# One maximum over two heads, scatters in twos, and norms recorded later, in a six-layer decoder kernel

## The chip, the cores and the metric

The kernel runs on one core of one Trainium2 chip. The metric is the device time of one execution in microseconds (us): the median of three runs. A separate execution was profiled; durations, waits and stretches of time come from that one. The core's engines run their own queues in order: TensorE (PE) for matmuls, VectorE (DVE), ScalarE (ACT), GpSimd (POOL), and SyncE (SP), which only issues transfers.

## The reference

Sixteen batches of 128 tokens with 512 features pass through six sublayers, each followed by a residual add and a layer norm: a state-space scan, a cross attention with heads of 128, a ternary feed-forward, and then the three that matter here.

```
# 4: causal self-attention, 16 query heads of 32 on 4 key heads, 8-bit activations, ternary weights
p = softmax(where(causal, -inf, q k^T / sqrt(32)));  x = norm(x + bitlinear(p v, Wo))
# 5: gated cross attention, 16 heads of 32, masked keys
p = softmax(where(mask, q k^T / sqrt(32), -inf));    x = norm(x + sigmoid(n wg) * ((p v) wo))
# 6: experts: 8 of 64 masks per token by softmax and top-k, grouped into 8 weight sets
w = top8(softmax(x gate));  per set g: xg = x + softmax(w_g) mask_up[g]
x = norm(x + sum_g sum(w_g) * (silu(xg G_g) * (xg U_g)) D_g)
```

## The kernel before, in words

The six sublayers are written as stages. The two small-head attentions share one stage, `stage_attention`. It makes eight `SelfAttention` objects and then eight `GatedAttention` objects, one for each pair of batches, and cuts each into eight units of four heads: unit `n` is batch `n // 4`, key head (or row group of 32 partitions) `n % 4`. A loop over a step number `t` records, for the units at several distances ("lags") from `t`, the pieces of a small pipeline:

- `scores(n)`, two steps ahead and for even `n` only: PE adds the mask by a matmul and multiplies queries and keys of two units, row groups side by side, into two PSUM tiles of one bank each, tagged `sc0` to `sc3`. `Side` keeps these matmuls in the written order, the second unit first.
- `top(n)`, one step ahead: DVE takes the maximum over keys of the four heads of one unit (L1001, L1170) and multiplies it by a negative scale (L1002, L1171).
- `exps(n)`: ACT makes four exponentials (L1010, L1178). In the self-attention POOL then adds up parts of the rows (L1013, L1014), which the values' step sums (L1043). In the gated one `norm(n)` follows: two small DVE steps (L1184, L1185), and POOL multiplies the whole unit (L1186).
- `turn(n)`: four transposes on PE into the only bank of the pool `ppt`, and a copy to SBUF, for odd `n` on ACT (L1025), for even `n` on DVE (L1027).
- `values(i)` after four units: PE multiplies by the values. In the self-attention ACT copies the result (L1041), DVE sums and inverts the row parts (L1043, L1044), PE turns it back and DVE scales it (L1050). In the gated one the output matmul follows, DVE multiplies by the gate (L1211), POOL adds it to the residual `x` (L1212), and after the second batch of a pair DVE makes the layer norm (`layernorm`, L61 to L72, whose first instruction is L68).

Python generators, advanced once per step (`yield`), hold the projections, values and outputs; so a `yield` sets at which step an instruction is recorded. That recording is not the final order: a scheduling layer below it places the instructions on each engine's queue, and only `Side` pins some of them.

From the middle of the gated attention on, `Moe` runs beside it. `route(p)` decides for one pair of batches of the first half which experts each token goes to; ACT copies the tokens into a row buffer `r_row` (L1453, four buffers, so two pairs), DVE fills in the weights (L1475 to L1477), and `scatter` (L1481) sends each of the two rows to eight expert buckets in DRAM by indirect transfers from POOL's queue (L1486), one per step. The second half of the batches is routed during the expert stage, `stage_moe`.

The expert stage loops over 98 tiles of 128 tokens, each a unit with fetch, masks, gate and up products, and the product with `dn` into `y`, which DVE copies to `yo` (L1549) and ACT's queue stores to DRAM. `combine` later gathers the results back (L1558, POOL's queue), and after three steps POOL adds them to `x` (L1565). After two steps more, for the last expert of the first half, `finish` makes a pair's final layer norm on DVE and sends the result out.

Of the kernel before, what the change touches and what calls it, by code (L numbers as in the profile page):

```python
# [10 lines left out]
F32 = mybir.dt.float32  # L11
# [5 lines left out]
ALU = mybir.AluOpType  # L17
AX = mybir.AxisListType
PSUM = bass.MemoryType.PSUM

P = 128
NB = 16
D = 512
KC = D // P
# [836 lines left out]
class SelfAttention:  # L861
# [4 lines left out]
    HD = 32  # L866
    SCALE = 1.0 / math.sqrt(HD)
    LAG = 1

    def __init__(self, k, p, pools):  # L870
        self.k, self.nc, self.xs = k, k.nc, k.x[2 * p : 2 * p + 2]
        self.wk, self.wr, self.pp, self.psc, self.ppt, self.pao = pools
        self.o, self.part, self.sT, self.s, self.sc, self.mx = [], [None, None], {}, {}, {}, {}

    def rope(self, ps, n, tag):
        nc, HD, tabs = self.nc, self.HD, self.k.bit_tabs
# [108 lines left out]
    def scores(self, n):  # L985

        nc, (i, g) = self.nc, divmod(n, 4)
        side = Side(self.k)
        scs = [self.psc.tile([P, 4, P], F32, tag=f"sc{g + e}", name="sc") for e in range(2)]
        for e in (1, 0):  # L990
            side(nc.tensor.matmul(scs[e], self.k.identb, self.k.bit_mask, start=True, stop=False))
        for j in range(4):
            for e in range(2):
                r = slice(32 * (g + e), 32 * (g + e) + 32)
                side(nc.tensor.matmul(scs[e][:, j], self.qT[i][r, j], self.kT[r, i], start=False, stop=j == 3))
        self.sc[n], self.sc[n + 1] = scs

    def top(self, n):
        nc = self.nc
        mx = self.mx[n] = self.k.small.tile([P, 4], F32, tag="mx", name="mx")  # L1000
        nc.vector.tensor_reduce(mx, self.sc[n], AX.X, ALU.max)  # L1001
        nc.vector.tensor_scalar(mx, mx, self.nal[:, n // 4 : n // 4 + 1], None, ALU.mult)  # L1002

    def exps(self, n):
        nc, (i, g) = self.nc, divmod(n, 4)
# [13 lines left out]
    def turn(self, n):  # L1019
        nc = self.nc  # L1020
        pt = self.ppt.tile([P, D], F32, tag="pt", name="pts")
        transpose4(self.k, pt, self.s[n].rearrange("p r t -> p (r t)"))
        sT = self.sT[n] = self.wk.tile([P, D], F32, tag="at_T", name="at_T", bufs=7)
        if n % 2:
            nc.scalar.copy(sT, pt)  # L1025
        else:
            nc.vector.tensor_copy(sT, pt)  # L1027

    def values(self, i):

        yield
        nc, wk = self.nc, self.wk
        ao = self.pao.tile([P, D], F32, tag="ao", name="ao")
        side = Side(self.k)
        for g in (3, 0, 1, 2):
            side(nc.tensor.matmul(
                ao[32 * g : 32 * g + 32], self.v[:, i, g * self.HD : (g + 1) * self.HD], self.sT[4 * i + g], start=True, stop=True
            ))
        yield
        aoT = wk.tile([P, D], F32, tag="aoT", name="aoT")  # L1040
        nc.scalar.copy(aoT, ao)  # L1041
        sm = self.k.small.tile([P, 4, 4], F32, tag="sm16", name="sm16")
        nc.vector.tensor_reduce(sm.rearrange("p j g -> p g j"), self.part[i], AX.X, ALU.add)  # L1043
        nc.vector.reciprocal(sm, sm)  # L1044
        yield
        po = self.pao.tile([P, 16, self.HD], F32, tag="ao", name="pao")
        transpose4(self.k, po.rearrange("p h f -> p (h f)"), aoT)
        yield
        o = self.wr.tile([P, 16, self.HD], F32, tag="so", name="so")
        nc.vector.tensor_tensor(o, po, sm.rearrange("p j g -> p (j g)").unsqueeze(2).to_broadcast([P, 16, self.HD]), ALU.mult)  # L1050
        self.o.append(o.rearrange("p h f -> p (h f)"))
        yield
        if i == 1:
            yield from self.output()
# [18 lines left out]
class GatedAttention:  # L1073
# [5 lines left out]
    HD = 32  # L1079
    SCALE = HD ** -0.5  # L1080
    LAG = 2

    def __init__(self, k, p, pools):
        self.k, self.nc, self.b0, self.xs = k, k.nc, 2 * p, k.x[2 * p : 2 * p + 2]
        self.wk, _, self.pp, self.psc, self.ppt, self.pao = pools
        self.sT, self.s, self.sc, self.mx, self.sm = {}, {}, {}, {}, {}

    def project(self):

# [62 lines left out]
    def scores(self, n):  # L1152
        nc, (i, r) = self.nc, divmod(n, 4)
        tok = slice(i * P, (i + 1) * P)
        side = Side(self.k)
        scs = [self.psc.tile([P, KC, P], F32, tag=f"sc{r + e}", name="sc") for e in range(2)]
        for e in (1, 0):
            side(nc.tensor.matmul(
                scs[e], self.k.identb, self.k.gated_mask[:, self.b0 + i].unsqueeze(1).to_broadcast([P, KC, P]), start=True, stop=False
            ))  # L1160
        for c in range(KC):
            for e in range(2):
                rows = slice(32 * (r + e), 32 * (r + e) + 32)
                side(nc.tensor.matmul(scs[e][:, c], self.qT[rows, c, tok], self.kT[rows, c, tok], start=False, stop=c == KC - 1))
        self.sc[n], self.sc[n + 1] = scs

    def top(self, n):
        nc = self.nc
        mx = self.mx[n] = self.k.small.tile([P, KC], F32, tag="mx", name="mx")
        nc.vector.tensor_reduce(mx, self.sc[n], AX.X, ALU.max)  # L1170
        nc.vector.tensor_scalar(mx, mx, self.r[:, 2, n // 4 : n // 4 + 1], None, ALU.mult)  # L1171

    def exps(self, n):
        nc, i = self.nc, n // 4
# [47 lines left out]
def stage_attention(k):  # L1222

    nc, tc = k.nc, k.tc
    U = 8
    with ExitStack() as ctx:
        wk = ctx.enter_context(tc.tile_pool(name="s4w", bufs=2))  # L1230
        own = ctx.enter_context(ExitStack())
        wr = own.enter_context(tc.tile_pool(name="s4r", bufs=2, side="right"))
        pp = ctx.enter_context(tc.tile_pool(name="s4p", bufs=2, space=PSUM))
        psc = ctx.enter_context(tc.tile_pool(name="s4s", bufs=1, space=PSUM))
        ppt = ctx.enter_context(tc.tile_pool(name="s4t", bufs=1, space=PSUM))
        pao = ctx.enter_context(tc.tile_pool(name="s4o", bufs=1, space=PSUM))
        pools = wk, wr, pp, psc, ppt, pao
        pairs = [c(k, p, pools) for c in (SelfAttention, GatedAttention) for p in range(NB // 2)]
        units = [(pr, n) for pr in pairs for n in range(U)]

        begin = {}
        for m, pr in enumerate(pairs):
            begin.setdefault(U * m - (14 if m < NB // 2 else 10), []).append(pr)
        running = [load_gated_weights(k)]
        first = [pairs[0].project(), pairs[1].project()]
        for n in range(12):
            next(first[0])
            if n >= 7:
                next(first[1])
        running.append(first[1])  # L1250
        for t in range(-2, len(units) + 2):
            if k.moe:
                k.moe.tick()
            for lag in (2, 1, 0, -1, -2):
                if not 0 <= t - lag < len(units):
                    continue
                pr, n = units[t - lag]
                if lag == pr.LAG:
                    pr.turn(n)
                    if n % 4 == 3:  # L1260
                        running.append(pr.values(n // 4))
                if lag == 1:
                    pr.norm(n)
                if lag == 0:
                    pr.exps(n)
                if lag == -1:
                    pr.top(n)
                if lag == -2 and n % 2 == 0:
                    pr.scores(n)
            if t == NB // 2 * U + 20:  # L1270
                own.close()
                k.moe = Moe(k, pp)
                running.append(k.moe.setup())
            for pr in begin.get(t, []):
                if t > -2:
                    running.append(pr.project())
            for job in list(running):
                if next(job, running) is running:
                    running.remove(job)
            if k.moe:  # L1280
                k.moe.tick()
                k.moe.send()
        while running:
            k.moe.tick()
            for job in list(running):
                if next(job, running) is running:
                    running.remove(job)
            k.moe.tick()
            k.moe.send()


class Moe:
# [188 lines left out]
    def scatter(self, p, rows, to):  # L1481
        k, nc, half = self.k, self.nc, p // (NB // 4)
        for i, row in enumerate(rows):
            nc.sync.dma_start(k.rows[2 * p + i], row)
            for g in range(self.NG - half):
# [1 line left out]
                    out=k.bucket[half][g][:, :], out_offset=bass.IndirectOffsetOnAxis(ap=to[:, i, g : g + 1], axis=0),  # L1487
                    in_=row[:, :], in_offset=None, bounds_check=self.CAP - 1, oob_is_err=False,
                )
                yield  # L1490


    def fetch(self, u):
# [58 lines left out]
    def combine(self, h, g, n):  # L1552

        k, nc, b = self.k, self.nc, h * (NB // 2) + n
# [8 lines left out]
        yield  # L1563
        yield
        nc.gpsimd.tensor_tensor(k.x[b], got, k.x[b], ALU.add)  # L1565
        yield
        yield
        if g == self.NG - 1 and n % 2:
            self.finish(b - 1)

# [215 lines left out]
```

## Time and profile before

| what | us |
|---|---|
| median of three runs | 3400.72 (3398.65 to 3407.02) |
| profiled execution | 3407.26 |
| its span, first to last instruction | 3405.5 |
| PE, DVE, ACT, POOL busy | 3172.3, 1894.7, 1373.7, 1391.6 |
| self-attention, about | 1960 to 2165 in the span |
| gated attention, about | 2165 to 2505 |
| experts | 2505 to the end |

The profile's row of slices divides the span into 40 equal parts with a digit for tenths of busy time. A group line gives the source line, engine, operation, output and input, count, then busy us, mean ns of one, and the idle time of the engine just before, with what ended it. A timeline line gives start, duration, engine, line and operation, and in brackets the idle time before and who ended it. A line of waits gives total us, times and the longest.

### The profile page before, as it was taken

To read this page: it belongs to the slowest core of one execution; us is meant where nothing else is said; L and a number is where in the kernel's file an instruction comes from. 1 tells how busy PE (TensorE), PEld (TensorE's weight loads), DVE (VectorE), ACT (ScalarE), POOL (GpSimd) and SP (SyncE) were. 2 spreads that over 40 slices of the span, in tenths; PEclk is the share of its full clock that TensorE was granted. 3 is DMA by queue.
4 is the path that set the end of the run, shared out by engine and by line. 5 is a ranking of instruction groups with operands and counts; after the bars stand their busy time and mean duration, and the time that the engine had idled before them with its cause. 6 is when DMAs were issued, how large, how long until landed. Compare 5 with 4: busy or idle time off the path is not lost. (4 is left out here: it accounts for less than half of the span.)

```text
span 3405.5 us, 38787 instructions
## 1 busy us (share of the span) xinstructions
PE 3172.3 (93%) x12944; PEld 1817.4 (53%) x12944; DVE 1894.7 (56%) x4346; ACT 1373.7 (40%) x3283; POOL 1391.6 (41%) x1198
## 2 busy tenths in 40 slices
PE   6888999899999999999799899998889999999998
PEld 3444444455555555555466465665555566556665
DVE  5877888456456456455576589765543232222223
ACT  4645655133233333335333388865543231111221
POOL 6967887243333233332000165224624455233331
PEclk8999999999999999999899999998989999999999
DMA  7887332200000000003100100013435566445441
GB/s 237 259 254 217 96 87 68 67 7 4 7 4 7 4 4 7 4 1 124 59 1 1 62 1 1 10 59 119 152 131 179 195 223 201 166 152 174 159 159 65
DMA packets 161554, 317.29 MB, mean 93 GB/s; under 512 B 19113, under 2 KB 82089, under 8 KB 158276
## 3 DMA queue, kind: packets, MB, share of 16 engines
q1 hardware_dynamic: 123012, 215.83, 20.6%
q0 software_dynamic: 19328, 64.56, 5.6%
q10 hardware_dynamic: 19008, 34.35, 2.7%
q8 instruction: 105, 1.72, 0.2%
q14 instruction: 101, 0.83, 0.1%
HBM read 238.80 MB, written 129.04 MB: 108 GB/s over the span
## 5 line engine op out<-in xcount | busy, mean ns | idle before, releaser
L245 POOL TENSOR_TENSOR dBx<-dtx,BC 128x1024 f32<-128x1024 f32 x128 | 301.6, 2375 | 45.4 <-DVE h L258 36.8
L1522 PE MATMUL pg<-gu,xgT 128*128 128x352 f32 x784 | 301.7, 467 | 0.0
L1522 PE MATMUL pu<-gu,xgT 128*128 128x352 f32 x784 | 300.6, 466 | 0.0
L1539 PE MATMUL y<-dn,aT 128*128 128x512 f32 x588 | 268.3, 592 | 0.0
L1526 DVE SCALAR_TENSOR_TENSOR act<-pu,row,act 128x352 f32<-128x352 f32 x98 | 57.1, 583 | 377.7 <-PE pu L1522 327.0
L575 POOL TENSOR_TENSOR pr<-pr,sm 128x512 f32<-128x512 f32 x128 | 134.7, 1053 | 287.9 <-DVE sm L574 242.5
L236 ACT ACTIVATE h<-dt,negA 128x254 f32<-128x254 f32 x512 | 239.8, 474 | 14.9 <-DVE dt L178 2.1
L1565 POOL TENSOR_TENSOR x<-got,x 128x512 f32<-128x512 f32 x120 | 152.7, 1277 | 226.0 <-DMA got<-results,gidx 225.2
L606 PE MATMUL po<-w,aT 128*128 128x512 f32 x512 | 230.5, 593 | 1.1 <-DVE aT L600 1.1
L483 PE MATMUL pq<-w,xT 128*128 128x512 f32 x512 | 228.9, 594 | 0.0
L1558 POOL DMA_INDIRECT got<-results,gidx x120 | 116.1, 968 | 269.8 <-DMA results<-yo 248.2
L258 DVE TENSOR_TENSOR_SCAN h<-h,dBx 128x1024 f32<-128x1024 f32 x80 | 183.0, 2294 | 71.1 <-ACT h L236 48.8
L460 POOL TENSOR_TENSOR m<-m,m 128x512 f32<-128x512 f32 x96 | 121.6, 1267 | 244.2 <-DVE m L455 244.2
L568 ACT ACTIVATE pr<-sc,mx,sf 128x256 f32<-128x256 f32 x256 | 142.8, 562 | 187.0 <-DVE mx L561 176.1
L267 PE MATMUL py<-hC,ident 128*128 128x512 f32 x320 | 167.3, 652 | 54.6 <-ACT y L272 48.9
L1522 PEld LDWEIGHTS pu<-gu,xgT 128*128 128x128 f32 x784 | 151.5, 193 | 85.2 <-issue 4.4
L1522 PEld LDWEIGHTS pg<-gu,xgT 128*128 128x128 f32 x784 | 143.9, 194 | 65.1 <-issue 3.9
L1525 ACT ACTIVATE act<-pg 128x352 f32<-128x352 f32 x98 | 45.5, 464 | 318.8 <-PE pg L1522 256.8
L1539 PEld LDWEIGHTS y<-dn,aT 128*128 128x128 f32 x588 | 104.1, 190 | 100.8 <-issue 94.2
L1514 ACT COPY xgT<-ptx 128x512 f32<-128x512 f32 x98 | 57.5, 587 | 234.7 <-PE ptx L375 213.3
L483 PEld LDWEIGHTS pq<-w,xT 128*128 128x128 f32 x512 | 93.5, 190 | 102.0 <-issue 99.0
L606 PEld LDWEIGHTS po<-w,aT 128*128 128x128 f32 x512 | 94.8, 190 | 95.8 <-issue 91.8
(363 smaller groups left out, 6851.0 us busy)
## 6 DMA issues: line engine op xcount, KB each, us to landing
bucket<-zeros SPq DMA_DIRECT2D x96, 388.0 KB
row<-bucket SPq DMA_DIRECT2D x90, 388.0 KB
BC<-bcd SPq DMA_DIRECT2D x128, 256.0 KB
results<-yo ACTq DMA_DIRECT2D x90, 256.0 KB
gu<-in_moe_guT SPq DMA_DIRECT2D x16, 1408.0 KB
cT<-in_ctxT SPq DMA_DIRECT2D x32, 256.0 KB
dn<-in_moe_downT SPq DMA_DIRECT2D x16, 512.0 KB
rows<-r_row SPq DMA_DIRECT2D x16, 388.0 KB
```

What stands on the lines that cost most here:

```text
L236: nc.scalar.activation(h[:, c, :, 1:], st.dt[:, c].rearrange("p (b t) -> p b t", b=BQ)[:, :, 1:], AF.Exp, scale=negA[:, c, n : n + 1])
L245: nc.gpsimd.tensor_tensor(dBx, st.dtx, BC[:, 0].unsqueeze(1).to_broadcast([P, KC, TQ]), ALU.mult)
L258: nc.vector.tensor_tensor_scan(hf, hf, df, 0.0, ALU.mult, ALU.add)
L267: nc.tensor.matmul(st.py[c], k.ident, st.hC[n][:, 2 * c : 2 * c + 2], start=n == 0, stop=n == NS - 1)
L460: nc.gpsimd.tensor_tensor(m1, m1, m2, ALU.add)
L483: nc.tensor.matmul(ps, src[:, c], w[c], start=c == 0, stop=c == KC - 1)
L568: nc.scalar.activation(pr[:, j], st.sc[g, i][:, j], AF.Exp, scale=st.sf[:, h : h + 1], bias=st.mx[g, i][:, j : j + 1], accum_out=sm[:, j : ...
L575: nc.gpsimd.tensor_tensor(pr, pr, sm.unsqueeze(2).to_broadcast([P, 2, 2 * P]), ALU.mult)
L606: nc.tensor.matmul(st.po, aT[:, j], k.wo[h // 8][:, h % 8], start=h == 0, stop=h == G * J - 1)
L1522: nc.tensor.matmul(ps, u.xT[:, c], gu[:, c, lo : lo + I], start=c == 0, stop=c == KC - 1)
L1539: self.nc.tensor.matmul(u.y, u.aT[:, c], u.w[1][:, c], start=c == 0, stop=c == 2)
L1565: nc.gpsimd.tensor_tensor(k.x[b], got, k.x[b], ALU.add)
```

## The change

The two heads' scores of a pair of units get one tile of two banks (tags `sc0` and `sc2`), and `top` is called for even `n` only, with one reduce over `128 x 2 x 4` rows of keys and one multiply for eight maxima. In the self-attention, three of four transposed units are copied by ACT instead of one of two (`DVE_TURNS` is 4 there and 2 in the gated attention), and the sum and inverse of the row parts are recorded one step later. `scatter` yields after every second transfer instead of each. `combine` waits four steps instead of two between its add and `finish`.

```diff
+    DVE_TURNS = 4
...
-        scs = [self.psc.tile([P, 4, P], F32, tag=f"sc{g + e}", name="sc") for e in range(2)]
+        both = self.sc2[n] = self.psc.tile([P, 2, 4, P], F32, tag=f"sc{g}", name="sc")
+        scs = [both[:, e] for e in range(2)]
...
-        mx = self.mx[n] = self.k.small.tile([P, 4], F32, tag="mx", name="mx")
-        nc.vector.tensor_reduce(mx, self.sc[n], AX.X, ALU.max)
+        mx = self.k.small.tile([P, 2, 4], F32, tag="mx", name="mx")
+        nc.vector.tensor_reduce(mx, self.sc2[n], AX.X, ALU.max)
         nc.vector.tensor_scalar(mx, mx, self.nal[:, n // 4 : n // 4 + 1], None, ALU.mult)
+        self.mx[n], self.mx[n + 1] = mx[:, 0], mx[:, 1]
...
-        if n % 2:
+        if n % self.DVE_TURNS:
             nc.scalar.copy(sT, pt)
         else:
             nc.vector.tensor_copy(sT, pt)
...
         aoT = wk.tile([P, D], F32, tag="aoT", name="aoT")
         nc.scalar.copy(aoT, ao)
+        yield
+        po = self.pao.tile([P, 16, self.HD], F32, tag="ao", name="pao")
+        transpose4(self.k, po.rearrange("p h f -> p (h f)"), aoT)
+        yield
         sm = self.k.small.tile([P, 4, 4], F32, tag="sm16", name="sm16")
         nc.vector.tensor_reduce(sm.rearrange("p j g -> p g j"), self.part[i], AX.X, ALU.add)
         nc.vector.reciprocal(sm, sm)
-        yield
-        po = self.pao.tile([P, 16, self.HD], F32, tag="ao", name="pao")
-        transpose4(self.k, po.rearrange("p h f -> p (h f)"), aoT)
-        yield
...
-                if lag == -1:
+                if lag == -1 and n % 2 == 0:
                     pr.top(n)
...
-                yield
+                if g % 2:
+                    yield
...
         nc.gpsimd.tensor_tensor(k.x[b], got, k.x[b], ALU.add)
-        yield
-        yield
+        for _ in range(4):
+            yield
         if g == self.NG - 1 and n % 2:
             self.finish(b - 1)
```

The gated attention's `scores` and `top` are changed in the same way (L1156 and L1168).

More of the change, by code (lines that the diff above doesn't have):

```diff
@@ L872, in __init__ @@
         self.wk, self.wr, self.pp, self.psc, self.ppt, self.pao = pools
-        self.o, self.part, self.sT, self.s, self.sc, self.mx = [], [None, None], {}, {}, {}, {}
+        self.o, self.part, self.sT, self.s, self.sc, self.sc2, self.mx = [], [None, None], {}, {}, {}, {}, {}
     def rope(self, ps, n, tag):
@@ L1041, in values @@
         nc.scalar.copy(aoT, ao)
-        sm = self.k.small.tile([P, 4, 4], F32, tag="sm16", name="sm16")
-        nc.vector.tensor_reduce(sm.rearrange("p j g -> p g j"), self.part[i], AX.X, ALU.add)
-        nc.vector.reciprocal(sm, sm)
         yield
@@ L1048, in values @@
         yield
+        sm = self.k.small.tile([P, 4, 4], F32, tag="sm16", name="sm16")
+        nc.vector.tensor_reduce(sm.rearrange("p j g -> p g j"), self.part[i], AX.X, ALU.add)
+        nc.vector.reciprocal(sm, sm)
         o = self.wr.tile([P, 16, self.HD], F32, tag="so", name="so")
@@ L1081 @@
     LAG = 2
+    DVE_TURNS = 2
     def __init__(self, k, p, pools):
@@ L1085, in __init__ @@
         self.wk, _, self.pp, self.psc, self.ppt, self.pao = pools
-        self.sT, self.s, self.sc, self.mx, self.sm = {}, {}, {}, {}, {}
+        self.sT, self.s, self.sc, self.sc2, self.mx, self.sm = {}, {}, {}, {}, {}, {}
     def project(self):
@@ L1155, in scores @@
         side = Side(self.k)
-        scs = [self.psc.tile([P, KC, P], F32, tag=f"sc{r + e}", name="sc") for e in range(2)]
+        both = self.sc2[n] = self.psc.tile([P, 2, KC, P], F32, tag=f"sc{r}", name="sc")
+        scs = [both[:, e] for e in range(2)]
         for e in (1, 0):
@@ L1168, in top @@
         nc = self.nc
-        mx = self.mx[n] = self.k.small.tile([P, KC], F32, tag="mx", name="mx")
-        nc.vector.tensor_reduce(mx, self.sc[n], AX.X, ALU.max)
+        mx = self.k.small.tile([P, 2, KC], F32, tag="mx", name="mx")
+        nc.vector.tensor_reduce(mx, self.sc2[n], AX.X, ALU.max)
         nc.vector.tensor_scalar(mx, mx, self.r[:, 2, n // 4 : n // 4 + 1], None, ALU.mult)
+        self.mx[n], self.mx[n + 1] = mx[:, 0], mx[:, 1]
     def exps(self, n):
```

## The prediction

> **What bounds the kernel now.** I read the page first: its row of slices shows TensorE (PE) at nine tenths or more almost everywhere, and the row under it the clock that it was granted.
>
> ```profile
> PE   6888999899999999999799899998889999999998
> PEclk8999999999999999999899999998989999999999
> ```
>
> A busy PE is not PE at its peak, so I then asked for busy times by stage. Columns: stretch, its length, busy us (instructions) of PE, PE weight loads, DVE (VectorE), ACT (ScalarE), POOL (GpSimd), PE clock, DMA.
>
> ```profile
> 1963.00:2163.00 200.00, 185.49 (x1364) 114.40 (x1364) 186.37 (x547) 163.58 (x394) 104.99 (x159) 0.96 0.00 1
> 2163.00:2503.00 340.00, 305.16 (x2016) 197.61 (x2018) 205.88 (x727) 218.68 (x666) 152.30 (x151) 0.92 0.25 88
> 2560.00:2720.00 160.00, 148.44 (x562) 91.91 (x561) 52.66 (x136) 46.83 (x92) 72.92 (x69) 0.96 0.56 187
> 2940.00:3005.00 65.00, 51.98 (x172) 30.18 (x171) 25.58 (x83) 8.79 (x23) 18.21 (x17) 0.92 0.47 160
> ```
>
> Row one is the self-attention. DVE is busy 186.4 of 200 us, and in half of its 10 us slices it is full while PE is at 7.4 to 9.5: DVE sets the pace, ACT follows at 82%. Row two is the gated attention: PE leads (305 of 340), and DVE and ACT have room on average, so its losses are single stalls. Rows three and four hold the experts' two stalls; between them PE is full (220 of 220).
>
> **Part 1: one maximum over two heads.** The groups and one stretch of DVE's timeline (start, us) price it.
>
> ```profile
> L259 DVE TENSOR_TENSOR hC<-h,BC 128x1024 f32<-128x1024 f32 x80 | 96.8, 1210 | 2.7 <-PE py L267 0.6
> L1001 DVE TENSOR_REDUCE mx<-sc 128x4 f32<-128x512 f32 x64 | 42.7, 680 | 19.8 <-PE sc L995 17.9 <-ACT at_s L1010 1.6
> L1002 DVE TENSOR_SCALAR mx<-mx,nal 128x4 f32<-128x4 f32 x64 | 20.9, 337 | 0.0
> L1025 ACT COPY at_T<-pts 128x512 f32<-128x512 f32 x64 | 37.8, 591 | 40.3 <-PE pts L375 40.1
> ```
> ```profile
> 2041.47 0.68 DVE L1001 TENSOR_REDUCE mx<-sc 128x4 f32<-128x512 f32 x1
> 2042.08 0.15 DVE L895 RECIPROCAL qs<-qs 128x2 f32<-128x2 f32 x1
> 2042.15 0.67 DVE L1027 COPY at_T<-pts 128x512 f32<-128x512 f32 x1
> 2042.73 0.15 DVE L896 TENSOR_SCALAR qs<-qs 128x2 f32<-128x2 f32 x1
> 2042.80 0.22 DVE L1002 TENSOR_SCALAR mx<-mx,nal 128x4 f32<-128x4 f32 x1
> ```
>
> Per pair of heads DVE did two reduces (1.28 us back to back at 2471.53) and two multiplies (0.35 at 2472.73). It will do one reduce of 1024 elements and one multiply of 8. No reduce over two banks is in this trace; the nearest row is the 1024-element product, 1.21 us. The multiply stays at 0.22. That saves 0.07 + 0.13 = 0.20 us. The mean multiply is 337 ns against 220 undisturbed (261 in the gated stage, L1171): 0.12 (0.04) of hold-up goes with each multiply removed. So 0.32 us a pair in the self-attention and 0.24 in the gated one; times 32 pairs, 10.2 and 7.7 us of DVE time.
>
> [...]
>
> Could the first head's exponentials start later? Before, DVE mostly ran both reduces and then both multiplies, so the first head already waited 1.28 + 0.2; now 1.21 + 0.2. The scores of a later pair were issued second head first, so they already waited for both heads' exponentials; the two-bank tile adds no wait. I put both at nothing; where the first reduce did stand alone, up to 0.5 us is lost on ACT, hidden as long as ACT has other exponentials queued.
>
> **Part 2: every fourth copy on DVE.** In the built program, DVE has 48 transposed-score copies instead of 64, and ACT 80 instead of 64. DVE loses 16 x 0.61 (start to start above) = 9.8 us; ACT gains 16 x 0.59 = 9.5.
>
> **Sum for the self-attention.** DVE 186.4 - 10.2 - 9.8 = 166.4; ACT 163.6 + 9.5 = 173.1, so ACT is late next. At the fill that the leading engine had (186.4 of 200, 0.93) the stage would take 186 us, 14 less. But two nearly equal queues that feed each other fill worse: at 0.91 it is 190, and I take **-10**. The moved sum of the parts (0.67 + 0.24 us of DVE, 16 times) costs nothing: four transposes on PE (0.6 us) stand in front of its only reader. If that cover were gone, 0.9 us would fall on a chain with a whole unit's slack.
>
> **The gated stage's share of part 1.** 7.7 of 206 us on an engine that is not the bound. DVE ended about 21 of the 34 us that PE idled there; 7.7/206 of a 340 us stage would be 13 us if DVE bound all of it, and a tenth to a fifth of that is reasonable: **-1.5**.
>
> **Part 3: rows sent two per part.** The scatters' number (120 of 0.98 us, 1.28 start to start) stays; their place on POOL changes. They pass POOL's head normalisations (L1186, 1.05 us) and its residual adds (L1212, 1.28 us). The timeline at the gated stage's last bad stall:
>
> ```profile
> 2462.93 0.98 POOL L1486 DMA_INDIRECT bucket<-r_row,r_to  x1 [0.30 <-issue]
> 2463.91 1.30 POOL L1212 TENSOR_TENSOR x<-x,gate 128x512 f32<-128x512 f32 x1
> 2465.24 0.69 DVE L68 BATCH_NORM_STATS2 ln_st<-x 128x6 f32<-128x512 f32 x1 [7.10 <-POOL x L1212]
> 2471.30 1.09 PE L375 MATMUL pts<-ident,at_s 128*128 128x128 f32 x4 [5.68 <-DVE at_T L1027]
> ```
>
> The add's input was ready at 2458.14 (L1211), but six scatters stood before it. DVE sat behind the add in the norm, the copy that PE needed sat behind the norm, and PE idled 5.7 us. In the new order two scatters stand directly before this add (batch 11), and one pair's 16 end before the next pair's begin. From this pair's first scatter (2431.1), 16 x 1.28 + six normalisations x 1.1 + one add = 28.4 us: the add starts at 2459.5, 4.4 us earlier. At the second stall (batch 7, add at 2370.9) 16 scatters and three normalisations from 2343.7 end at 2367.7, about 3 earlier; ACT's 3.8 us wait at 2368 for a row buffer goes, since the earlier pair's rows are then long gone. Against that, batch 5's add gets 15 scatters before it instead of eight: 2299.6 + 15 x 1.28 + 2 x 1.05 = 2320.9 instead of 2317.7, **+3**. Batch 9 stays.
>
> A stall also costs clock:
>
> ```profile
> 2474.00:2476.00 2.00, 2.00 (x14) 1.67 (x16) 0.69 (x1) 1.99 (x9) 0.00 (x0) 0.50 0.00 0
> ```
>
> The two-microsecond rows show about 0.5 from 2469.5 to 2478.5: 9 us at half speed lose 4.6. [...] I use the row, and count half of it once, since a shorter idle may still trip it: -4.4 - 3 + 3 - 2.3 = -6.7, rounded down to **-5** because PE does not gain all that POOL does. Ends: -18 (both stalls and their half clock gone) and +8 (batch 5's delay becomes a stall of its own).
>
> **Part 4: later norms beside the experts.** DVE waits 36.8 us (7 times, to 8.1) in a norm (L68) for POOL's add (L1565); PE makes 67 fewer matmuls in 2950 to 3000 than its pace of 38 per 10 us, 17.6 us lost. But the yields only move the point of recording. In the built program DVE's order from the first expert on is the same, and so are PE's, ACT's and SP's; on POOL four adds move by one scatter. The norm still stands directly before the copy that empties `y`. Value **0**; likewise the scatters beside the experts and the stalls of row three.
>
> **Sum.** -10 - 1.5 - 5 = -16.5 on the profiled execution, 3407.26 us (span 3405.5 and 1.8 around it). That execution lies 6.5 above the median of 3400.7; taken off the median: **3384**.
>
> **Rivals.**
> - *ACT takes the place of DVE (same).* ACT must make three copies in four, each behind exponentials in its queue (0.39 us each, groups of four), into a transposed-score bank of which there is one. For: ACT ends at 173 of the old 200 and PE already waited 8.7 us for its copies in the gated stage. Against: DVE drops by 20 us. Self -3, the rest -1: 3397.
> - *POOL bursts (slower).* With 16 scatters in a row, every residual add whose gate is ready more than two scatters (2.6 us) before POOL is free makes a stall like the shown one: 5.7 idle + 4.6 of half clock = 10.3 us. For: POOL is 80% busy in the slices after a route ends. If batches 5 and 9 become such and 7 and 11 stay: +20.6 - 10 = +11, 3412.
> - *The norms do move.* If the wait of row four vanished: -17.6 more, 3366. Against: the order on every queue.
>
> **Chances.** Forecast 0.62; ACT 0.21; POOL bursts 0.13; norms 0.04. About 0.3% (10.2 us) is what a measurement can tell from no change. Faster: nine tenths of the forecast (0.56) and the norms, 0.60; same: ACT's case and 0.05 of the forecast's weak edge, 0.26; slower: the bursts and the last 0.01, 0.14. The range runs from both stalls with their clock gone and the stage at 0.93 (-14 - 3 - 18 = -35, 3366) to +5, a mild burst (3406).
>
> **What would show it.** Right: self-attention near 190 us, DVE near 166 and ACT near 173 in it; a two-bank reduce near 1.2 us, 32 in each attention; no 7 us wait of L68 for batch 11's add; row four unchanged, with its 36.8 us wait. Wrong: a reduce above 1.36, ACT full in the self-attention, L68 waiting for batches 5 and 9, half clock in more slices, or a PE without idle at 2940 to 3005.

## The result, and the profile after

The changed kernel takes 3381.5 us (median of six runs, 3375.7 to 3387.6) against 3402.3 for the kernel before on the same chip (3398.1 to 3407.0): ratio 0.9936, 95% interval 0.9925 to 0.9946. That is 0.6% faster, some 21 us; the forecast was 3384. The profiled execution took 3382.4 us, with a span of 3380.6.

First the profile's two rows of slices, after:

```profile
PE   6888999899999999999799989998989999989998
PEclk8999999899999999999899989999999999999999
```

The digits differ from those of before in a few slices, some of them downwards, because the slices are shorter and cut elsewhere: they are too coarse for a change of half a per cent. So the stages are cut at landmarks that each kernel has: from the self-attention's first exponential to the gated attention's first, from there to the experts' first gate product, and on to their last. The stretches of before, with the columns of the prediction (length; busy us of PE, weight loads, DVE, ACT, POOL; clock; DMA):

```profile
1966.80:2169.90 203.10, 187.16 (x1394) 116.06 (x1394) 187.65 (x545) 168.24 (x402) 106.79 (x163) 0.97 0.00 1
2169.90:2517.70 347.80, 307.42 (x2017) 197.86 (x2015) 207.98 (x739) 213.54 (x659) 151.98 (x149) 0.92 0.26 92
2517.70:3384.90 867.20, 842.61 (x3131) 515.97 (x3132) 250.75 (x557) 199.13 (x434) 324.09 (x296) 0.98 0.52 172
```

And the same three of after:

```profile
1968.90:2158.20 189.30, 175.06 (x1378) 114.47 (x1397) 169.51 (x466) 174.12 (x417) 105.95 (x163) 0.99 0.01 1
2158.20:2494.00 335.80, 301.36 (x2008) 194.77 (x2011) 203.42 (x676) 213.00 (x659) 151.90 (x149) 0.94 0.27 95
2494.00:3360.00 866.00, 841.53 (x3130) 516.19 (x3131) 250.12 (x557) 199.54 (x434) 323.67 (x296) 0.98 0.52 173
```

The self-attention is 13.8 us shorter, the gated stage 12.0, the experts 1.2; with a start that is 2.1 later this makes the 24.9 us between the two spans. That is more than the medians' 21, since the profiled execution of before lay some 5 us above its median and that of after 1.

One execution's stage carries noise. In five kernels below whose gated attention is made by the same code (the changed kernel is one of them; two have more row buffers) the gated stage took 335.8, 337.1, 339.7, 340.1 and 343.6 us; the self-attention took 189.2 to 189.4 in the four whose self-attention is the same too. Most of the gated stage's spread lies in one place. Batch 4's residual add is the last ahead of the first scatter; here the stage is cut there, before and then after:

```profile
2169.90:2292.95 123.05, 114.56 (x774) 75.47 (x773) 80.84 (x281) 89.64 (x278) 34.51 (x36) 0.96 0.16 46
2292.95:2517.70 224.75, 192.86 (x1245) 122.39 (x1243) 127.14 (x460) 123.90 (x382) 117.47 (x114) 0.90 0.31 116
```
```profile
2158.20:2276.55 118.35, 110.08 (x760) 72.71 (x764) 76.23 (x251) 88.75 (x276) 33.33 (x36) 0.99 0.17 48
2276.55:2494.00 217.45, 191.28 (x1251) 122.06 (x1248) 127.19 (x426) 124.25 (x383) 118.56 (x114) 0.91 0.33 121
```

In the five kernels the first part takes 117.9 to 125.5 us, at a clock of 0.99 down to 0.93, and the second 217.4 to 219.2. So of the 12.0 us that the stage is shorter, 4.7 lie ahead of every scatter, where kernels of the same code differ by more, and 7.3 behind.

The groups of after that answer to part 1 and to the moved copies:

```profile
L1028 ACT COPY at_T<-pts 128x512 f32<-128x512 f32 x80 | 48.8, 610 | 21.3 <-PE pts L375 19.9 <-issue 1.2 <-remote 0.2
L1003 DVE TENSOR_REDUCE mx<-sc 128x8 f32<-128x1024 f32 x32 | 38.6, 1206 | 18.3 <-PE sc L997 18.3
L1004 DVE TENSOR_SCALAR mx<-mx,nal 128x8 f32<-128x8 f32 x32 | 12.8, 399 | 0.1
```

The two-bank reduce takes 1206 ns, as the 1024-element product had suggested (1210). Halving their number took 4.1 us of busy time from the reduces (42.7 before) and 8.1 from the multiplies (20.9 before).

Batch 11's residual add, whose wait was the last bad stall of before, in the timeline of after:

```profile
2440.99 0.69 DVE L1217 TENSOR_TENSOR gate<-pw,gate 128x512 f32<-128x512 f32 x1 [0.49 <-PE pw L1214]
2441.94 0.97 POOL L1492 DMA_INDIRECT bucket<-r_row,r_to  x1 [0.30 <-issue]
2442.93 1.28 POOL L1218 TENSOR_TENSOR x<-x,gate 128x512 f32<-128x512 f32 x1
2444.25 0.69 DVE L68 BATCH_NORM_STATS2 ln_st<-x 128x6 f32<-128x512 f32 x1 [2.56 <-POOL x L1218]
2450.27 0.94 PE L375 MATMUL pts<-ident,at_s 128*128 128x128 f32 x4 [2.47 <-DVE at_T L1030]
```

The add starts 1.3 us after its input is ready instead of 5.8, DVE waits 2.6 us instead of 7.1, and PE 2.5 instead of 5.7. Over the stage, the norms' waits for POOL's adds, before and after (total us, times, longest):

```profile
DVE ln_st L68 <- POOL x L1212: 26.8, 10, 7.1
DVE ln_st L68 <- POOL x L1218: 16.0, 9, 3.1
```

Part 4's wait, in the lists of waits, is where it was; the first line is of before, and the last is ACT's wait for a row buffer in the changed kernel:

```profile
DVE ln_st L68 <- POOL x L1565: 36.8, 7, 8.1
DVE ln_st L68 <- POOL x L1572: 38.1, 7, 8.4
ACT r_row L1459 <- DMA bucket<-r_row,r_to: 34.0, 4, 12.1
```

### The profile page after: what moved, and what is told of

Its sections match the earlier page's. It is cut to its first block, busy times and chain, and to the rows that moved or that the text cites. A ratio compares the mean times of both kernels' runs of the same rounds, so it can differ in the third digit from the quotient of the medians.

```text
span 3380.6 us, 38522 instructions
## 1 busy us (share of the span) xinstructions
PE 3153.0 (93%) x12894; PEld 1813.6 (54%) x12944; DVE 1876.7 (56%) x4202; ACT 1379.5 (41%) x3299; POOL 1389.5 (41%) x1198
## 5 line engine op out<-in xcount | busy, mean ns | idle before, releaser
L258 DVE TENSOR_TENSOR_SCAN h<-h,dBx 128x1024 f32<-128x1024 f32 x80 | 183.0, 2294 | 71.0 <-ACT h L236 48.7
```

The lines of the kernel that those rows point to most:

```text
L258: nc.vector.tensor_tensor_scan(hf, hf, df, 0.0, ALU.mult, ALU.add)
```

## The experiments

All ratios are to the kernel before, timed on the same chip, with the 95% interval; 0.001 is 3.4 us. The stages come from one profiled execution each, cut as above.

| kernel | ratio | self | gated | experts |
|---|---|---|---|---|
| before | 1 | 203.1 | 347.8 | 867.2 |
| changed | 0.9936 (0.9925 to 0.9946) | 189.3 | 335.8 | 866.0 |
| e_max | 0.9975 (0.9966 to 0.9985) | 192.4 | 353.6 | 864.4 |
| e_turns | 0.9976 (0.9965 to 0.9986) | 197.2 | 342.9 | 867.6 |
| e_scatter | 0.9975 (0.9965 to 0.9985) | 204.5 | 340.3 | 863.5 |
| e_norms | 0.9991 (0.9982 to 1.0000) | 205.6 | 346.2 | 866.3 |
| e_nogmax | 0.9934 (0.9920 to 0.9947) | 188.5 | 340.0 | 865.7 |
| e_noscatter | 0.9956 (0.9943 to 0.9970) | 189.4 | 343.4 | 868.6 |
| e_pin | 0.9880 (0.9865 to 0.9896) | 189.4 | 339.7 | 847.9 |
| e_rrow8 | 0.9891 (0.9875 to 0.9906) | 189.2 | 337.1 | 850.3 |
| e_pin_rrow | 0.9839 (0.9826 to 0.9852) | 189.2 | 340.1 | 831.6 |
| e_burst | 1.0042 (1.0030 to 1.0055) | 189.4 | 369.6 | 869.3 |
| e_turns8 | 0.9949 (0.9937 to 0.9961) | 189.1 | 343.6 | 864.7 |
| e_addv | 0.9780 (0.9766 to 0.9793) | 189.3 | 316.0 | 832.3 |

My theory was the prediction's own: DVE's relief shortens the self-attention until ACT is late, the scatters' order takes two stalls out of the gated stage, and the norms do nothing, because their order does not change. The rivals were ACT as the new bound and POOL's bursts.

### Each part alone: e_max, e_turns, e_scatter, e_norms

Four kernels make one part of the change each, on the kernel before. e_max has the two-bank tile and the merged maximum in both attentions, as in the diff of the change. e_turns moves the copies:

```diff
+    DVE_TURNS = 4
...
-        if n % 2:
+        if n % self.DVE_TURNS:
```

e_scatter sends two rows per step:

```diff
-                yield
+                if g % 2:
+                    yield
```

e_norms waits two steps more:

```diff
-        yield
-        yield
+        for _ in range(4):
+            yield
```

> The kernel before with only the merged maximum (two-bank tiles, one reduce and one multiply for two heads). Theory (DVE sets the pace of the self-attention): DVE loses 8 to 10 us there, so the stretch from the first self-attention exponential to the first gated one shrinks from 203 us by 5 to 9; the gated stage by 1 to 4; the experts by nothing; total ratio 0.997 to 0.999. Rival (the gated stage's gain of the whole change comes from the merged maximum and not from the scatters): the gated stretch shrinks from 348 us by 8 or more, total ratio below 0.996. Rival (latency: the first head now waits for both): ratio 1.000 or above.

> The kernel before with only DVE_TURNS = 4 in the self-attention. Theory (DVE sets the pace, ACT has room): DVE loses 9.8 us, ACT gains 9.5, self-attention shorter by 4 to 8 us, other stretches unchanged, ratio 0.998 to 0.999. Rival (ACT becomes the bound, the single transposed-score bank waits for ACT): no gain or a loss, ratio 1.000 to 1.002, and more PE wait for the ACT copy.

> The kernel before with only two scatters per part. Theory (a residual add behind six scatters blocks DVE, then PE, then the clock): no 7 us wait of a norm for the residual add, self-attention unchanged at 203 us, gated stretch shorter by 5 to 9 us, experts unchanged, ratio 0.9975 to 0.9985. Rival (POOL bursts): gated stretch longer, ratio above 1. Rival (gain comes from the maximum): within 2 us, ratio 0.9995 to 1.0005.

> The kernel before with only the two more yields ahead of the final norms. Theory (the scheduler puts the norms where they were): every queue has the same order, the wait of the norms for POOL's add stays at 36 to 39 us, ratio 1.000 within 0.001. Rival (the norms do move): the wait goes, ratio about 0.995.

Three parts gain about 8.5 us each; the fourth 3 us, with an interval that reaches down to nothing. In e_max the self-attention's DVE is busy 176.8 us, 10.9 less than before, and the stage is 10.7 shorter. In e_turns DVE is 6.9 us less busy and the stage 5.9 shorter. The two gains add to 16.6 alone and are 13.8 together. e_max's gated stage came out 5.8 us longer in its one profile, an execution 5.2 us above its kernel's median; e_nogmax looks into it. e_scatter gains in the gated stage, and its 3.7 us among the experts is not repeated by the changed kernel (1.2). The order of PE's queue is the same in e_scatter as before; on DVE and ACT a few steps of norms and routes moved with the scatters. e_norms has the same order as before on every queue. By the product of the four ratios the whole would be 0.9917. It is 0.9936; the 3 us in the self-attention are a part of that difference, and the intervals cover the rest.

### Take one part away: e_nogmax, e_noscatter

In the changed kernel, e_nogmax takes the gated maxima head by head again, on the halves of the two-bank tile:

```diff
-        mx = self.k.small.tile([P, 2, KC], F32, tag="mx", name="mx")
-        nc.vector.tensor_reduce(mx, self.sc2[n], AX.X, ALU.max)
+        mx = self.mx[n] = self.k.small.tile([P, KC], F32, tag="mg", name="mx")
+        nc.vector.tensor_reduce(mx, self.sc[n], AX.X, ALU.max)
...
-                if lag == -1 and n % 2 == 0:
+                if lag == -1 and (n % 2 == 0 or pr.LAG == 2):
```

e_noscatter goes back to one row per step:

```diff
-                if g % 2:
-                    yield
+                yield
```

> The changed kernel, with the gated attention's maxima taken one head at a time again (two reduces and two multiplies on the halves of the same two-bank tile). Theory A, the prediction's: the merged maximum is worth about 1.5 us in the gated stage, since DVE is not its bound; ratio to before about 0.9940, gated stage about 337 us. Rival B: the merged maximum hurts there, as the gated stage of the kernel with the maxima alone was 5.8 us longer than before; then the stage gets shorter without it, about 330 us, ratio about 0.992. Rival C: DVE does bound it after all; then about 8 us come back, ratio about 0.996.

> The changed kernel, with one scatter per step again. Theory A, the prediction's: the order of the scatters is worth 5 us in the gated stage and nothing beside the experts; ratio to before about 0.9951, gated stage about 341 us, with a wait of about 7 us of a norm for a residual add back in it. Rival B: it is worth the 8 to 9 us that it gave alone, a part of it beside the experts; ratio about 0.9962. Rival C: the stalls depend on where the other engines happen to stand, so that the scatters' gain is gone once the attention is faster; ratio within 0.001 of the changed kernel's 0.9936.

e_nogmax runs at 0.9934, the changed kernel at 0.9936: the merged maximum neither helps nor hurts the gated stage by an amount that can be measured. Rival C's 0.996 is outside the interval. Rival B's 0.992 is its lower edge, but the shorter stage that B asks for is not there (340.0 us, within the spread of the stage). e_max's 353.6 is thus no price of the maximum in the changed kernel; what made it is open. e_noscatter gives back 0.0020, about 7 us, between theory A's 5 and rival B's 9; the intervals of the two ratios just overlap. The 7 us wait of batch 11's norm is back, in its list of waits:

```profile
DVE ln_st L68 <- POOL x L1218: 24.4, 9, 7.7
```

It was 16.0 us in the changed kernel, with 3.1 as the longest. Where the order counts shows when the gated stage is cut at residual adds (us, one execution each):

| kernel | scatters a step | start to batch 4's add | to batch 7's | to batch 11's | to the experts |
|---|---|---|---|---|---|
| before | 1 | 123.0 | 78.0 | 93.0 | 53.8 |
| e_max | 1 | 124.7 | 77.5 | 97.8 | 53.7 |
| e_noscatter | 1 | 121.3 | 71.3 | 97.3 | 53.5 |
| e_scatter | 2 | 125.5 | 75.4 | 88.4 | 51.1 |
| changed | 2 | 118.4 | 78.5 | 87.9 | 51.1 |
| e_pin | 2 | 121.1 | 76.8 | 87.8 | 54.1 |
| e_turns8 | 2 | 125.5 | 76.1 | 87.9 | 54.2 |

Between the adds of batches 7 and 11 every kernel with one scatter a step takes 93.0 us or more (e_turns and e_norms 93.2 both), and every one with two 88.4 or less. In the other columns the two kinds overlap. From batch 4's add to the experts PE idles 31.9 us before and 26.2 in the changed kernel; its busy time hardly differs (192.9 and 191.3).

### The norms, moved in fact: e_pin; the row buffers: e_rrow8; both: e_pin_rrow

The fourth part moved only the point of recording. On the changed kernel, e_pin keeps the first instruction of these norms (those that `finish` makes from `combine`) in the written order, so that they stand at expert tiles 54 to 59 instead of 46 to 51:

```diff
-        nc.vector.bn_stats(st, r)
+        ins_ = nc.vector.bn_stats(st, r)
+        if pin:
+            k.tc.keep_in_program_order(ins_)
...
-            self.finish(b - 1)
+            self.finish(b - 1, True)
```

e_rrow8 takes away ACT's wait for a row buffer:

```diff
-        rows = [wr.tile([P, self.ROW], F32, tag="r_row", name="r_row", bufs=4) for _ in range(2)]
+        rows = [wr.tile([P, self.ROW], F32, tag="r_row", name="r_row", bufs=8) for _ in range(2)]
```

> The changed kernel, with the first instruction of the later norms kept in the written order, so that they really move from expert tiles 46 to 51 to tiles 54 to 59. Theory A, the prediction's reading of the fourth part: the edit gave nothing because the order on the queues stayed; with the norms moved, the 38 us in which DVE waits for the adds go, and PE's stall of some 17 us at 2920 to 2980 with them: experts about 850 us, ratio to before about 0.989. Rival B: PE's stall there is fed by something else too (the gathers, the rows' transfers), and only a part goes: experts 858 to 862, ratio about 0.992. Rival C: nothing, the wait is replaced by the next one: 0.9936.

> The changed kernel, with eight row buffers instead of four, so that ACT's copy of a pair's rows never waits for the scatters of the pair two before. Theory A: ACT's 34 us of waits for row buffers stand in front of work that PE needs beside the experts (the stalls at 2580 to 2600 and 2660 to 2680); without them the experts get 8 to 15 us shorter: ratio to before about 0.990. Rival B: those stalls come from POOL and DVE (the norms and routes of the second half); then the waits go, and the experts stay within 2 us: ratio 0.9936.

> The changed kernel with both: the later norms really moved, and eight row buffers. The first alone gave ratio 0.988 to before, the second alone 0.9891, against the changed kernel's 0.9936, and each took away a stall of PE at another place (2900 to 3000, and 2580 to 2680). Theory A: the two add up, 19 and 15 us off the changed kernel: experts about 832 us, ratio to before about 0.9835. Rival B: a part of each is won from the same slack (the last expert's rows and the gathers at the end), and together they give no more than 22 us: ratio 0.987.

Three stretches of the experts in the changed kernel, where PE is not full:

```profile
2500.00:2600.00 100.00, 95.53 (x372) 60.16 (x371) 39.83 (x87) 30.89 (x62) 36.93 (x35) 0.97 0.54 182
2600.00:2700.00 100.00, 94.42 (x369) 59.32 (x368) 30.70 (x79) 29.81 (x59) 43.83 (x42) 0.97 0.59 198
...
2900.00:3000.00 100.00, 85.60 (x304) 51.46 (x302) 33.48 (x97) 15.79 (x38) 29.04 (x26) 0.95 0.47 156
```

The last of them in e_pin:

```profile
2900.00:3000.00 100.00, 100.00 (x367) 60.74 (x366) 29.88 (x68) 19.81 (x48) 34.94 (x32) 1.00 0.52 171
```

And the first two in e_rrow8:

```profile
2500.00:2600.00 100.00, 100.00 (x409) 63.68 (x408) 41.43 (x92) 31.99 (x65) 36.16 (x34) 1.00 0.57 192
2600.00:2700.00 100.00, 100.00 (x392) 62.13 (x391) 33.59 (x101) 32.16 (x61) 51.26 (x49) 1.00 0.64 218
```

In each kernel exactly the stall that it aimed at is gone: PE is full, at the full clock, and makes 63 and 60 more matmuls in the stretch. In the lists of waits the 38.1 us of e_pin's norms and the 34.0 us of e_rrow8's row copies do not appear any more. The row copies of e_rrow8 now wait for the norm that makes their rows (30.0 us, against 10.5), without a stall of PE in these stretches. e_pin gains 0.0056 on the changed kernel (19 us), e_rrow8 0.0045 (15 us), and both together 0.0097 (33 us): theory A's sum holds, and rival B's shared slack is out. The experts of e_pin_rrow take 831.6 us, with PE busy for 831.4 of them.

### A rival provoked: e_burst

```diff
-                if g % 2:
+                if g % 8 == 7:
```

> The changed kernel, with a yield only after all eight transfers of a row, so that 8 to 16 scatters stand in a row on POOL, ahead of several residual adds. Theory A, the prediction's rival of the bursts: an add that waits behind more than two scatters stalls PE, by some 5 us and some clock; gated stage 345 us or more, ratio to before 0.9965 or more. Rival B: what counts is that a pair's scatters are over before the next norm needs POOL; then the bursts cost nothing, gated stage 333 to 338 us, ratio 0.993 to 0.994. The waits of a norm for the residual add tell which: over 6 us each in A, under 4 in B.

It is 0.0106 above the changed kernel, some 36 us, and the gated stage is 34 us longer. The time agrees with theory A, but its mark is missing: the norms wait for POOL's adds for 8.6 us in all, 1.9 at most. The timeline shows one of the losses. Between 2346 and 2356 POOL issues eight scatters in a row:

```profile
2345.12 1.06 POOL L1192 TENSOR_TENSOR at_s<-at_s,sm 128x512 f32<-128x512 f32 x1
...
2355.18 0.59 ACT L1210 COPY oT<-ao 128x512 f32<-128x512 f32 x1 [12.32 <-remote]
2356.33 3.04 POOL L1192 TENSOR_TENSOR at_s<-at_s,sm 128x512 f32<-128x512 f32 x3
2358.64 5.15 PE L1136 MATMUL pg<-x_wg,xT 128*128 128x512 f32 x8 [8.46 <-ACT r_x L1398]
2361.44 0.18 DVE L1190 RECIPROCAL sm<-sm 128x4 f32<-128x4 f32 x1 [14.07 <-ACT at_s L1184]
```

Three head normalisations stand behind the scatters and run at once when these end. ACT sat idle for 12.3 us and PE for 8.5. What released ACT's copy at 2355.18 the trace calls only "remote"; PE had made the product that it copies by 2347. So time goes beside the burst, but which hand-over carries it to ACT is left open. Nor is it the bursts alone that e_burst changes: transposes and scores stand in another order on PE's queue in places, and small steps of norms on DVE's.

### Is ACT the next bound? e_turns8

```diff
-    DVE_TURNS = 4
+    DVE_TURNS = 8
```

> The changed kernel, with seven of eight transposed units of the self-attention copied by ACT instead of three of four: eight copies go from DVE to ACT. Theory A: DVE and ACT are level now (169.5 and 174.1 of 189.3 us), so ACT becomes the bound at about 179 of a stage of 192 to 195; ratio to before about 0.995. Rival B: DVE still sets the pace, as it is DVE whose maxima and copies the others wait for; DVE falls to about 164.5 and the stage to about 186; ratio about 0.9925. Rival C: neither does, PE's own order holds the stage at 189: ratio 0.9936 within 0.0005.

The self-attention of this kernel:

```profile
1962.90:2152.00 189.10, 175.97 (x1395) 113.62 (x1393) 165.84 (x458) 176.55 (x426) 104.56 (x161) 0.99 0.01 1
```

DVE is 3.7 us less busy and ACT 2.4 more, and the stage does not move (189.1 to 189.3). In the stage, rival C's number holds: neither ACT's queue nor DVE's sets the pace alone. Since the copies only went from one to the other, a chain through both is not excluded. Nor do the rows show PE as the one that sets it: PE was busy for 0.92 of the stage before too (187.2 of 203.1 us), and for the same matmuls its busy time fell by 11 us with the stage (187.2 to 176.0), more than the 4 us or so that the clock would make by the rows (0.97 and 0.99), so that it may hold some waiting. What sets the 189 us is open. The ratio, 0.9949, would fit theory A, but its loss is not in the self-attention: the profile has it in the gated stage, ahead of the first scatter (125.5 us at a clock of 0.93, where the changed kernel has 118.4 at 0.99). The interval overlaps the changed kernel's. Yet all six executions have a clock of 0.963 or 0.964 over the span, against 0.965 to 0.968 in the changed kernel's six, so the loss may be real; its cause is open.

### The adds on DVE: e_addv

Built on e_pin_rrow, with PE's order unchanged:

```diff
-        nc.gpsimd.tensor_tensor(self.xs[i], self.xs[i], gt, ALU.add)
+        nc.vector.tensor_tensor(self.xs[i], self.xs[i], gt, ALU.add)
```

> The changed kernel with the later norms really moved and eight row buffers (ratio 0.9839 to before, gated stage 340.1 us), and the gated attention's 16 residual adds made by DVE instead of POOL, so that none of them stands behind scatters; PE's order is the same. Theory A, the prediction's: it is the add's place behind the scatters that makes the stalls; then the 16 us in which a norm waits for POOL's add go, the gated stage becomes about 333 us, ratio to before about 0.982, even though DVE gets 16 x 0.69 = 11 us more work in the stage. Rival B: POOL's head normalisations behind the scatters make them, as in the kernel with the bursts; then the wait for the add is exchanged for DVE's own adds, the stage stays at 340 to 344, ratio 0.984 to 0.985.

The gated stage of e_pin_rrow, and then of e_addv:

```profile
2154.70:2494.80 340.10, 306.65 (x2011) 197.22 (x2011) 203.68 (x676) 215.24 (x663) 151.97 (x149) 0.92 0.27 94
```
```profile
2151.90:2467.90 316.00, 291.43 (x2008) 189.71 (x2011) 210.34 (x692) 215.15 (x663) 132.54 (x133) 0.96 0.29 101
```

The stage is 24 us shorter, where theory A had 7. PE's idle time (length less busy) falls by 8.9 us, from 33.4 to 24.6; the other 15.2 are PE busy time for the same matmuls, as the clock goes from 0.92 to 0.96 (an estimate from the two rows: 340.1 x 0.08 = 27.2 us lost to the clock, against 316.0 x 0.04 = 12.6). Not all of this is sure: 5.6 us lie ahead of the first scatter (115.6 us at a clock of 1.00, against 121.2 at 0.96), where kernels of one code differ as much, and e_addv's profiled execution lay 5 us below its median. By the ratios it is 20 us ahead of e_pin_rrow. From batch 4's add on it takes 200.4 us instead of 218.9: 8.4 less idle time and 10.1 less PE busy time, with the clock at 0.94 instead of 0.90.

The 16 adds took 1273 ns each on POOL in e_pin_rrow and 794 on DVE in e_addv (medians 1272 and 692). That difference alone (7.7 us of engine time) would not have told of 20. This run takes away three things at once: the add's place behind the scatters, 20.4 us of POOL's time, and a hand-over from DVE to POOL and back. Over fifty of DVE's small steps, of norms and head sums above all, also stand elsewhere in its queue. The run shows the sum of these, not their shares.

e_addv is the fastest kernel of the study: 3327.8 us against 3400.6, 2.2% faster than before and 1.6% faster than the changed one.

## Why the prediction came out right, step by step

**The self-attention, -10: the mechanism right as far as DVE goes, the size short, and the 190 us in part luck.** e_max confirms DVE's 10.2 us of the merged maxima (10.9 measured). That a removed multiply takes its hold-up along is not shown by itself: in the changed kernel the mean multiply lies 167 ns above its median, before 115. By whole durations (2 x 0.68 - 1.21 + 0.34 = 0.49 us a pair) it would have been 15.6, by start-to-start gaps 4.5: 0.07 a pair for the reduces (1.28 - 1.21) and 0.07 for the multiply, as L1027 starts 0.07 us after an L895 of 0.15. In the same rows L895 starts 0.61 us after a reduce of 0.68, so that a whole duration is not what lies between two starts. The moved copies were priced too high: in e_turns each took 0.43 us from DVE (6.9 in all) and gave ACT 0.42 (6.7), where the prediction had 0.61 and 0.59. DVE ended at 169.5 us instead of 166.4, ACT at 174.1 (173.1). The stage ended at 189.3, near the forecast 190, because errors cancelled. The 200 us between round marks hold 163.6 of the 168.2 us that ACT is busy between the stage's own landmarks, which lie 203.1 apart. With these, the same working gives (168.2 + 9.5) / 0.91 = 195 us, a gain of 8. The 0.91, for two nearly equal queues, was the author's estimate. Measured, ACT rose by 5.9 only and filled 0.92 of the stage, as much as DVE had before, and the gain is 13.8. The wrong reason in it is "ACT is late next": e_turns8 loads ACT further, and the stage stays.

A term that the prediction did not have in this stage is the clock. It was 0.95 to 0.97 in the three kernels with the old self-attention (before, e_scatter, e_norms) and 0.99 or 1.00 in all others. By the rows, 203.1 x 0.03 = 6.1 us went to it before and 189.3 x 0.01 = 1.9 after: some 4 of the 13.8. The rows give the clock to 0.01, which is 2 us, so this is a rough estimate.

**The merged maximum in the gated stage, -1.5: right as small.** e_nogmax finds no difference. The 7.7 us of DVE time behind it were not tested alone: DVE's busy time in the stage fell by 3.7 in e_max, and by 4.6 with the whole change.

**The scatters, -5: the mechanism right at batch 11, the size near.** e_noscatter puts them at 7 us inside the change, e_scatter at 8.5 alone. Counted from batch 4's add, the last ahead of the first scatter, the changed kernel reaches batch 5's add 5.4 us later (predicted 3 later), batch 7's about half a us later, batch 11's 4.6 earlier (predicted 4.4), and the experts 7.3 earlier. So the 3 us foreseen for batch 7 are not there by themselves: batch 5's delay uses them up, as the prediction's own +3 and -3 cancel. In e_scatter the same four are 4.0 later, and 2.6, 7.2 and 9.9 earlier. The clock, which the prediction put at 2.3 us, is not shown: from batch 4's add on it is 0.90 before and 0.89 to 0.91 in the five kernels with the changed code, and PE's busy time is 192.9 before and 191.3 to 193.4 in them. The gain is mostly idle time (31.9 us before, 26.2 after). The 4.6 us for the half clock was itself read too high, since in the stretch from 2469.5 to 2478.5 PE was still idle until 2471.3: 7.2 us of work at the row's clock of 0.50 lose 3.6, by the prediction's own way of estimating. That a shorter idle can be followed by half clock too, for which the prediction kept 2.3 of the 4.6, the changed kernel shows once: behind PE's wait of 2.5 us at batch 11 the clock is 0.50 to 0.60 from 2450.3 to 2453.5.

**The later norms, 0: right, for the reason given.** In e_norms the order on every queue is that of before, the wait stayed (37.4 us there, 38.1 in the changed kernel), and the ratio is 0.9991, with 1 at the edge of its interval. Once the norms really move, in e_pin, the 17.6 us that the prediction laid on this stall come out as 19. Its rival "the norms do move", at 3366, thus had the right price (e_pin ran at 3362) for something that this change does not do.

**The rivals.** ACT as the bound is refuted in its stage by e_turns8. The bursts' price of +11 on the kernel before was near (e_burst is 0.0042 above it, 14 us), for an edit with eight or more scatters in a row, and what they hold up there is not the residual add as the rival said. In the changed order the seven in a row before batch 5's add do delay it; its norm waits 5.3 us in e_pin and e_rrow8, and in the changed kernel's profile no norm waits more than 3.1.

The sum of the steps was -16.5 us, the measured gain about 21. In the profiles the self-attention gave 3.8 us more than forecast and the part behind batch 4's add 2.3 more; the 4.7 ahead of it, at the higher clock (0.99 against 0.96), were not forecast and are within what kernels of one code differ by.

## What to carry to other kernels

Check in the built order of each queue whether an edit of the source moves anything: here the edit that moved nothing was worth nothing, and the same idea, made to hold, was worth 19 us. Look at TensorE's busy time for the same matmuls, and at its granted clock, beside its idle time: in e_addv more than half of what the stage gained was busy time. But cut a stage at landmarks inside it, and hold several kernels of the same code side by side, before a change in the clock is put down to an edit. And where an engine's work in order is mixed with slow issues (here scatters of 0.98 us, one every 1.28), look first at whether the small step that everybody waits for needs to be on that engine at all.

## What the runs showed of the hardware that was not expected

- With 16 adds of 1.27 us made by DVE instead of POOL, PE's busy time for the same matmuls was 10 us shorter from batch 4's add on (193.1 to 183.0), with the granted clock at 0.94 instead of 0.90.
- The same instructions on PE, after the same wait of 1.41 us, got another clock in another kernel. The changed kernel and e_pin have one order on every queue in the gated stage; here are 10 us of it in the first, with the output's eight matmuls, and then the same in e_pin:

```profile
2228.20:2238.20 10.00, 8.59 (x50) 5.65 (x49) 7.88 (x21) 9.10 (x31) 2.38 (x3) 1.00 0.01 2
2230.71 0.63 PE L375 MATMUL pts<-ident,at_s 128*128 128x128 f32 x4 [1.41 <-ACT at_T L1028]
2232.58 3.70 PE L1214 MATMUL pw<-x_wo,oT 128*128 128x512 f32 x8
```
```profile
2226.50:2236.50 10.00, 8.59 (x41) 4.70 (x40) 7.39 (x17) 8.80 (x31) 2.08 (x2) 0.83 0.01 2
2228.48 0.63 PE L377 MATMUL pts<-ident,at_s 128*128 128x128 f32 x4 [1.41 <-ACT at_T L1030]
2230.34 5.40 PE L1216 MATMUL pw<-x_wo,oT 128*128 128x512 f32 x8
```

  The eight took 3.70 us at a clock of 1.00 and 5.40 at 0.83. The wait before that one was 1.5 us in the first and 1.1 in the second. Why the clock fell in the one and not in the other is open.
- With eight scatters and more in a row on POOL (e_burst), PE idled 13.2 us in 18 pieces of up to 3.0 us in front of the values' matmuls, ended by nothing that the trace shows; the changed kernel has no such wait in the stage. All stand between 2343 and 2347, 2401 and 2410, or 2452 and 2461, within a burst or right behind it. Why is open.
- A small multiply's mean went from 337 ns for 4 elements to 399 for 8, while their number halved. Most of that is not its own work: the medians are 222 and 232 ns.
